# Attention of a block-sparse kernel: every unit gets its own order, and the pair items new places

## The chip, the cores and the metric

The kernel runs on one core of a Trainium2 chip. The core has TensorE (PE, with its weight loads shown apart as PEld), VectorE (DVE), ScalarE (ACT), GpSimd (POOL) and SyncE (SP, which here only issues transfers); each works through its own instructions in program order and waits for the others by semaphores. The metric is the device time of one execution in microseconds. What is compared is the median of several runs.

## The reference

The input X is 4 sequences of 2048 tokens with 256 features. It goes through an attention with 16 heads of 16 features, a layer norm, a mixture of experts and a second layer norm. Only the attention is touched:

```python
low = jnp.einsum('bnd,bmd->bnm', Qh, Kh) * SCALE          # means of blocks of 32 tokens
row_max = low.max(-1, keepdims=True)
norm = low - row_max + band * 5000.0                      # the three near blocks always
top_vals, idx = jax.lax.top_k(norm.reshape(Bm, n * n), NUM_BLOCK)   # 256 pairs a head
hi = jnp.einsum('bnqd,bnkd->bnqk', Qs, Ks) * SCALE        # chosen pairs, exactly
max_vals = full(-1e9).at[bidx, qblk].max(hi.max(-1))
attn = jnp.exp(hi - max_vals[bidx, qblk][..., None])
hi_out  = zeros.at[bidx, qblk].add(attn @ Vs)
hi_norm = zeros.at[bidx, qblk].add(attn.sum(-1))
low_attn = jnp.exp(low - row_max - 10000.0 * hi_mask) * BLK   # all other pairs, coarsely
out = (hi_out * hi_corr + low_out * low_corr) / (hi_norm * hi_corr + low_norm * low_corr + 1e-6)
```

Each head has 64 blocks of queries and of keys. The band (a block with itself and its two neighbours) holds 190 pairs, always chosen; the other 66 pairs of a head depend on the data.

## The kernel before, in words

`prepare` projects X to Q, K and V, makes the coarse scores and picks the pairs. `attend` (line 1164 on) is the attention. `experts` follows.

`attend` works on groups g = 0 to 15, each of four heads of one sequence; four groups make a batch (one sequence). A group has NU = 8 units of 256 tokens. The band is computed per unit in four steps:

- `row_max` (m, line 1294): 32 matmuls write the band's scores to `pa`, which is four PSUM banks and exists once; DVE reduces them to the maxima `m`.
- `scores` (s, line 1330), 8 units later: the scores again, turned and with the maximum subtracted by one more row of the operands, into `pa`; ACT takes the exponential into `e`. The profile calls `pa` `pm` in the first use and `ps` in the second.
- `values` (v, line 1356), one unit later: e times V into columns 0 to 255 of the bank `po`; ACT copies them to `oT`.
- `turn_values` (t, line 1378), one more unit later: two transposes of `oT` into columns 256 to 511 of `po`, and a copy from there into `ob`.

Between m and s, `lay_max` (line 1317) turns half a group's maxima (`pmt`, copied by ACT to `mt`) and SP writes them as a row into the query operand (`qt<-mt`, four transfers).

The pairs outside the band lie in OT = 9 tiles a batch, called pair tiles, k = 9 * batch + t. A pair tile passes through these items:

- `fetch` (line 1390): three gathers by POOL, of queries and keys into the one tile `gt`, of values into `gv`.
- `lay` (line 1407): SP writes each half of `gt` to DRAM (`scr`). `take` (line 1419): SP reads it back in another layout, four transfers into `qo` for part 0 and four into `kbd` for part 1. There are two sets of `qo` and `kbd`.
- `off_scores` (line 1440): two halves of 64 matmuls each into `pS`; after the second, DVE takes the maxima.
- `off_exp` (line 1464): DVE subtracts into `eo`, ACT takes the exponential in place, DVE turns the small maxima. `off_turn` (line 1478): DVE transposes `eo` to `eT`.
- `off_v` (line 1486): DVE transposes `gv` to `vt`, POOL copies it in four pieces into `vbd`.
- `off_values` (line 1496): two halves of 32 matmuls into `pO` (the same PSUM tile as `pS`), then ACT copies to `obo`, and the maxima go to a list through `pr`. `off_store` (line 1526): DVE transposes `obo` into the sums `o`.

Per group, one group later, `off_pen`, `off_scan`, `off_weights` and `off_scale` (lines 1530 to 1590) scale the pairs' sums (POOL multiplies `o`), `off_hot` (line 1591) makes the one-hot `hot` in two parts on DVE, and `off_sum` (line 1608) adds the pairs of a block by matmul (`ph`) in four parts. Two groups later `merge_exp`, `merge_weights`, `merge_band` and `merge_end` (lines 1670 to 1728) combine band, pairs and coarse part; `merge_weights` gives POOL three products over 128 x 1024, `merge_end` lets SP store the result (`att<-res`).

The order of all this is written out by hand. `plan` is a list of slots, two for each unit (TURN = 16 a group); `put` appends an item to a slot; `quiet` moves an item on past slots that hold `off_scores`. In a unit the loop at line 1833 issues m, t, the even slot (A), s, v, the odd slot (B), in this order in every unit. The items of a pair tile repeat every 7 slots with fixed distances: off_scores at 0 and 1, `take` of the tile two further on at 5 and 6, so that a tile's transfers are issued 8 slots before its off_scores. All engines receive their instructions in this one order, the transfers of SP among them.

Of the kernel before, what the change touches and what calls it, by code (L numbers as in the profile page):

```python
# [635 lines left out]
OT = (4 * NOFF + 31) // 32  # L636
# [527 lines left out]
def attend(tc, c, dram, keep, att, fills):  # L1164
# [5 lines left out]
    pe, dve, act, pool, sp = (  # L1170
        InOrder(tc, e) for e in (nc.tensor, nc.vector, nc.scalar, nc.gpsimd, nc.sync)
    )

    def matmul(*args, **kw):
        return pe.matmul(*args, start=True, stop=True, **kw)

    rows_of = [dram[n].rearrange("n (h d) q -> (n h) (d q)", d=HD) for n in ("tabq", "tabk", "tabv")]
    NU = L // 256
# [4 lines left out]
    GALL = 4 * B  # L1183
    with ExitStack() as st:
# [41 lines left out]
        NO = 2  # L1226
# [16 lines left out]
        def begin(g):  # L1243
            groups[g] = {
                "q": qts[g % NQ],
                "k": kts[g % NQ],
                "m": p3.tile([P, 2, 4, 8], F32, tag="m", name=f"m{g}"),
                "ob": p2.tile([P, 16, 4, 17], F32, tag="ob", name=f"ob{g}"),
            }
# [44 lines left out]
        def row_max(g, u):  # L1294

            s = groups[g]
            pa = ps4.tile([P, 4, 512], F32, tag="pa", name=f"pm{g}_{u}")
            for w in range(2):
                for n in range(2):
                    for j in range(4):  # L1300

                        cc = (n + j) % 2
                        t0 = 256 * u + 128 * w + 64 * cc
                        rows = slice(32 * j, 32 * j + KROWS)
                        matmul(
                            pa[64 * cc : 64 * cc + 64, j, P * w : P * w + P],
                            lhsT=s["q"][rows, t0 : t0 + 64],
                            rhs=s["k"][rows, t0 : t0 + P],
                        )
            dve.tensor_reduce(  # L1310
                s["m"][:, u // 4, :, 2 * (u % 4) : 2 * (u % 4) + 2],
                pa[:, :, 0:256].rearrange("p j (w k) -> p j w k", k=P),
                axis=AX.X,
                op=ALU.max,
            )
# [14 lines left out]
        def scores(g, u):  # L1330

            s = groups[g]
            pa = ps4.tile([P, 4, 512], F32, tag="pa", name=f"ps{g}_{u}")
            spans = [(2 * u + 1, 0, -64, 192), (2 * u + 2, 192, -64, 192)]
            n = 384
            if u == 0:
                spans.append((0, 384, 0, 128))
            elif u == NU - 1:
                spans[1], n = (2 * u + 2, 192, -64, 64), 256
            for x, o, t0, m in spans:  # L1340
                for j in range(4):
                    rows = slice(32 * j, 32 * j + KFULL)
                    matmul(
                        pa[:, j, o : o + m],
                        lhsT=s["k"][rows, P * x : P * x + P],
                        rhs=s["q"][rows, P * x + t0 : P * x + t0 + m],
                    )
            e = p3.tile([P, 4, 384], F32, tag="e", name=f"e{g}_{u}")
            act.activation(e[:, :, 0:n], pa[:, :, 0:n], AF.Exp, scale=0.25)
            s["e", u] = e  # L1350
            if u == 0:
                e0 = p1.tile([P, 4, P], F32, tag="e0", name=f"e0_{g}")
                act.activation(e0, pa[:, :, 384:512], AF.Exp, scale=0.25)
                s["e0"] = e0
# [23 lines left out]
        def turn_values(g, u):  # L1378
            s = groups[g]
            oT = s.pop(("oT", u))  # L1380
            for w in range(2):
                pe.transpose(po[:, 256 + P * w : 256 + P * w + P], oT[:, P * w : P * w + P], ident)
            dve.tensor_copy(
                s["ob"][:, 2 * u : 2 * u + 2],
                po[:, 256:512].rearrange("p (w j d) -> p w j d", w=2, j=4)[:, :, :, 0:17],
            )
# [342 lines left out]

        TURN = 2 * NU
        plan = [[] for _ in range(TURN * (GALL + 3))]

        def put(slot, f, *args):
            plan[slot].append((f, args))


        OWN = {  # L1740
            0: (0, 3, (6, 9, 10, 13)),
            1: (4, 7, (11, 14, 15, 18)),
            2: (2, 5, (9, 12, 13, 16)),
            3: (0, 3, (7, 10, 11, 14)),
        }
        for g in range(0, GALL, 4):
            z, b, i = TURN * g, g // 4, g % 4
            if g < GALL and i == 0:
                for t in range(OT):
                    k, at = b * OT + t, z + 7 * t  # L1750
                    put(at, off_scores, k, 0)
                    put(at + 2, fetch, k + NO, 0)
                    put(at + 1, off_v, k)
                    put(at + 3, fetch, k + NO, 1)
                    put(at + 1, off_scores, k, 1)
                    put(at + 2, off_exp, k)
                    put(at + 3, fetch, k + NO, 2)
                    put(at + 3, off_turn, k)
                    put(at + 4, lay, k + NO, 0)
                    put(at + 4, off_values, k, 0)  # L1760
                    put(at + 5, lay, k + NO, 1)
                    put(at + 5, off_values, k, 1)
                    put(at + 5, take, k + NO, 0)
                    put(at + 6, off_store, k)
                    put(at + 6, take, k + NO, 1)


        dense = {n for n, items in enumerate(plan) if any(f is off_scores for f, _ in items)}
# [1 line left out]
        def quiet(slot, f, *args):  # L1770
            while slot in dense:
                slot += 1
            put(slot, f, *args)
# [3 lines left out]
        for g in range(GALL + 2):  # L1777
            z, b, i = TURN * g, g // 4, g % 4
            if g < GALL:
                put(z + 11, lay_max, g, 0)  # L1780
                put(z + TURN + 2, lay_max, g, 1)

                if g + 1 < GALL:
                    for n in range(8):
                        quiet(z + n + 2, load, g + 1, n)
            if 0 < g <= GALL:
                scan, scale, at = OWN[i]
                put(z + scan, off_pen, g - 1)
                put(z + scan, off_scan, g - 1)
                put(z + scan + 1, off_weights, g - 1)  # L1790
                put(z + scale, off_scale, g - 1)
                put(z + at[0] - 2, off_hot, g - 1, 0)
                put(z + at[0] - 1, off_hot, g - 1, 1)
                for part in range(4):
                    put(z + at[part], off_sum, g - 1, part)
                if g % 2 == 1:
                    for part in range(4):
                        quiet(z + 2 + 2 * part, load_v, g - 1, 1, part)
            if g < GALL and g % 2 == 0:
                for part in range(4):  # L1800
                    quiet(z + 11 + part, load_v, g, 0, part)
            if g > 1:
                put(z + 8, merge_exp, g - 2)
                put(z + 9, merge_weights, g - 2)
                put(z + 11, merge_band, g - 2)
                quiet(z + 12, merge_end, g - 2)
            if 0 < g <= GALL:
                for cc in range(4):
                    quiet(z + 13 + cc, load_low, g - 1, cc)

        for n, f in enumerate(fills):
            quiet(TURN * 6 + n * TURN * 10 // len(fills), f, sp)

        lists = {}
        begin(0)
        patterns(0)
# [16 lines left out]
        for u in range(TURN // 2 * (GALL + 2)):  # L1833
            g = u // NU
            if u % NU == 0 and g + 1 < GALL:
                begin(g + 1)

            us, uv, ut = u - NU, u - NU - 1, u - NU - 2
            if g < GALL:
                row_max(g, u % NU)  # L1840
            if u % (4 * NU) == 0 and g < GALL:
                lists[g // 4] = p2.tile([P, OT * 32], F32, tag="r", name=f"r{g // 4}")
            if 0 <= ut < NU * GALL:
                turn_values(ut // NU, ut % NU)
            for f, args in plan[2 * u]:
                f(*args)
            if 0 <= us < NU * GALL:
                scores(us // NU, us % NU)
            if 0 <= uv < NU * GALL:
                values(uv // NU, uv % NU)  # L1850
            for f, args in plan[2 * u + 1]:
                f(*args)


NE = E - 1
# [630 lines left out]
def kernel(ctx: ExitStack, tc, x, wq, bq, wk, bk, wv, bv, *rest):  # L2486
# [24 lines left out]
    with tc.tile_pool(name="keepf", bufs=1) as kf:  # L2511
# [29 lines left out]
        with tc.If(flag == 1) as arms:  # L2541
            attend(tc, c, dram, keep, att, fills)
# [64 lines left out]
```

## Time and profile before

| what | us |
|---|---|
| runs (median; lowest, highest) | 1894.5 (1884.0, 1901.2) |
| profiled execution | 1891.8 |
| its span, first to last instruction | 1889.9 |
| busy over the span: PE, DVE, POOL, ACT | 1479.3, 1196.7, 727.0, 691.3 |
| first reduction of row maxima, last one | starts at 340.9 and 1222.2 |
| from one group's first reduction to the next, groups 1 to 14 | 51.3 to 59.2 |

A busy engine of the page is one that has an instruction in flight. In a row of groups the columns are: the engine and operation, what it writes and reads with shapes, how often, then the total busy time in us, the mean of one in ns, and the idle time just before these instructions with who ended it. A row of waits names the waiting engine and its output, whom it waited for, then us in total, how often, and the longest. Tile numbers are left out of the names, and most rows name line 654, which is the helper that keeps program order, so a group is known by its tiles.

### The profile page before, as it was taken

The numbers are of one execution on the slowest core, as the hardware profiler recorded it, in microseconds if no ns is written. First come the engines' busy times: TensorE is split into PE (matmuls) and PEld (weight loads), VectorE is DVE, ScalarE is ACT, GpSimd is POOL, SyncE is SP. The second block draws the span as 40 slices with busy tenths as digits, with TensorE's granted clock in tenths as the row PEclk, the third lists the DMA queues.
The fourth block names the chain that finished last, engine by engine and source line by source line (L and its number), as shares of the span: only waits on it lengthen the run. The fifth ranks groups of instructions, "written<-read, shape, count | busy, mean of one in ns | idle before, by whom it ended". The sixth has DMA issues, their size and how long they took to land.

```text
span 1889.9 us, 53418 instructions
## 1 busy us (share of the span) xinstructions
PE 1479.3 (78%) x21871; PEld 1064.3 (56%) x21871; DVE 1196.7 (63%) x3058; ACT 691.3 (37%) x1139; POOL 727.0 (38%) x731
## 2 busy tenths in 40 slices
PE   6787884348888778787887788863999998999980
PEld 4433442236666566566666566642557776788770
DVE  5478402537776667677776677742887558745775
ACT  3333332013333333333333333332454444544552
POOL 0100001213555535545543445333255434656355
PEclk9998997568887789898888878875999999999995
DMA  8699998668675968879788697416546565669885
GB/s 227 145 208 200 194 197 184 112 117 139 125 136 97 156 123 164 166 142 168 122 166 150 133 169 138 101 27 196 184 152 221 168 218 181 217 227 293 263 303 160
DMA packets 638763, 320.78 MB, mean 170 GB/s; under 512 B 468768, under 2 KB 601520, under 8 KB 636336
## 3 DMA queue, kind: packets, MB, share of 16 engines
q1 hardware_dynamic: 483136, 216.09, 52.0%
q0 software_dynamic: 21696, 63.50, 12.2%
q10 hardware_dynamic: 133680, 37.69, 8.6%
q8 instruction: 177, 2.90, 0.8%
q14 instruction: 74, 0.61, 0.1%
HBM read 165.33 MB, written 151.31 MB: 168 GB/s over the span
## 4 chain that ended last, share of the span: by engine, by line
PE 43%; DMA 19%; DVE 17%; issue 6%; SPq 4%; ACT 4%; POOL 3%; ACTq 3%; POOLq 0%; DVEq 0%
PE gu L654 6%; SPq L654 4%; PE po L654 4%; PE ps L654 4%; DMA tabq<-pj 3%; PE gp L654 3%; PE sy L654 3%; PE pp L654 3%; PE ph L654 3%; DVE m L654 3%; ACTq L654 3%; PE pm L654 3%; DMA vw<-v 2%; PE sT L654 2%; DMA xt<-in_L_attn_X_dram 2%
## 5 line engine op out<-in xcount | busy, mean ns | idle before, releaser
L654 ACT ACTIVATE e<-ps 128x1536 f32<-128x1536 f32 x144 | 186.2, 1304 | 299.3 <-PE ps L654 299.2
L654 POOL COPY vbd<-vt 32x512 f32<-32x512 f32 x144 | 94.2, 654 | 342.7 <-DVE vt L654 302.2
L654 DVE TENSOR_REDUCE m<-pm 128x8 f32<-128x1024 f32 x128 | 155.9, 1218 | 99.1 <-PE pm L654 98.5
L654 PE MATMUL ps<-qt,kt 26*128 26x192 f32 (+2 forms) x2176 | 151.4, 397 | 64.4 <-DVE m L654 55.5
L2250 POOL DMA_INDIRECT xs<-dx,pos x128 | 126.4, 988 | 146.5 <-issue 74.3
L654 PE MATMUL pp<-xT,wt 128*128 128x512 f32 x384 | 180.1, 617 | 3.4 <-ACT pj L654 3.4
L654 PE MATMUL gu<-guw,sxT 128*128 x736 | 176.9, 382 | 6.2 <-ACT sxT L654 4.7
L654 PE MATMUL pm<-kt,qt 25*64 25x128 f32 x4096 | 113.9, 320 | 65.9 <-ACT e L654 34.4
L654 POOL DMA_INDIRECT y<-ys,back x128 | 124.6, 974 | 105.6 <-DMA ys<-ysb 25.9
L654 PEld LDWEIGHTS ps<-qt,kt 26*128 26x128 f32 x2176 | 109.0, 220 | 94.4 <-DVE m L654 73.6
L654 PEld LDWEIGHTS gu<-guw,sxT 128*128 128x128 f32 x736 | 132.2, 191 | 25.6 <-ACT sxT L654 6.6
L654 PE MATMUL po<-e,vw 128*17 128x128 f32 (+1 forms) x4096 | 137.0, 284 | 10.4 <-issue 5.8
L654 PEld LDWEIGHTS po<-e,vw 128*17 128x17 f32 x4096 | 102.7, 111 | 51.5 <-issue 23.3
L654 PEld LDWEIGHTS pm<-kt,qt 25*64 25x64 f32 x4096 | 74.3, 152 | 95.2 <-ACT e L654 44.6
L654 PE MATMUL ph<-o,hot 128*128 128x256 f32 (+1 forms) x384 | 113.6, 431 | 16.5 <-ACT mt L654 10.5
L654 PEld LDWEIGHTS pp<-xT,wt 128*128 128x128 f32 x384 | 73.2, 200 | 84.0 <-issue 75.4
L654 ACT ACTIVATE pj<-pp,bt 128x512 f32<-128x512 f32 x96 | 65.5, 687 | 140.1 <-PE pp L654 68.4
L654 PE MATMUL pS<-kbd,qo 64*32 64x64 f32 x4608 | 71.2, 244 | 50.0 <-issue 20.0
L654 PE MATMUL sy<-dwt,shT 128*128 x368 | 97.7, 389 | 7.8 <-DVE shT L654 4.9
L654 POOL TENSOR_TENSOR o<-o,moT 128x544 f32<-128x544 f32 (+3 forms) x52 | 76.5, 1487 | 62.2 <-DMA gt<-tabq,rows 31.3
L654 ACT ACTIVATE eo<-eo 128x1024 f32<-128x1024 f32 x36 | 38.1, 1059 | 161.7 <-DVE eo L654 108.0
L654 PEld LDWEIGHTS ph<-o,hot 128*128 128x128 f32 x384 | 72.0, 203 | 38.1 <-ACT mt L654 9.2
(343 smaller groups left out, 2979.5 us busy)
## 6 DMA issues: line engine op xcount, KB each, us to landing
xr<-xs SPq DMA_DIRECT2D x92, 256.0 KB
ys<-ysb SPq DMA_DIRECT2D x92, 256.0 KB
scr<-gt SPq DMA_DIRECT2D x72, 256.0 KB
xs<-zero SPq DMA_DIRECT2D x108, 128.0 KB
qo<-scr SPq DMA_DIRECT2D x144, 64.0 KB
kbd<-scr SPq DMA_DIRECT2D x144, 64.0 KB
lt<-low SPq DMA_DIRECT2D x64, 144.0 KB
v<-vt ACTq DMA_DIRECT2D x16, 544.0 KB
```

The costliest lines, as they stand in the source:

```text
L654: return lambda *args, **kw: self.tc.keep_in_program_order(op(*args, **kw))
L2250: d = nc.gpsimd.indirect_dma_start(out=xs[i % 2], out_offset=bass.IndirectOffsetOnAxis(ap=s["pos"][:, k, t : t + 1], axis=0), in_=s["x1"][ ...
```

## The change

The instructions stay the same but for one: the copy from `po` to `ob` in `turn_values` is done by ACT in place of DVE. All else is order. Each of the 32 units of a batch has its own order of m, t, s, v, A and B (`ORDER`). The items of the nine pair tiles of a batch are put at slots listed one by one (`TILES`: off_scores twice, off_exp, off_turn, off_v, off_values twice, off_store, then three `fetch`, two `lay`, two `take` of the tile two further on). The per-group items get new slots: in `OWN`, for off_scan, off_scale, off_hot twice and off_sum four times; lay_max moves from 11 to 8 and from TURN + 2 to TURN + 1, merge_exp from 8 to 6, merge_end from 12 to 13. PSUM tiles, buffers and their numbers are unchanged.

```diff
@@ turn_values
-            dve.tensor_copy(
+            act.copy(
                 s["ob"][:, 2 * u : 2 * u + 2],
@@ attend, the plan
-        plan = [[] for _ in range(TURN * (GALL + 3))]
+        plan = [[] for _ in range(TURN * (GALL + 4))]
...
         OWN = {
-            0: (0, 3, (6, 9, 10, 13)),
-            1: (4, 7, (11, 14, 15, 18)),
-            2: (2, 5, (9, 12, 13, 16)),
-            3: (0, 3, (7, 10, 11, 14)),
+            0: (0, 3, 4, 4, 7, 10, 11, 16),
+            1: (3, 6, 7, 8, 10, 13, 16, 20),
+            2: (3, 5, 7, 8, 10, 13, 16, 19),
+            3: (1, 4, 4, 5, 9, 10, 11, 14),
         }
+        TILES = (
+            (1, 2, 2, 4, 1, 5, 6, 9, 0, 1, 3, 6, 7, 7, 8),
+            (8, 10, 10, 11, 7, 12, 13, 19, 10, 11, 11, 11, 12, 20, 21),
+            (14, 15, 16, 17, 13, 18, 19, 21, 11, 12, 20, 14, 15, 18, 19),
+            (21, 21, 24, 25, 22, 27, 27, 27, 24, 25, 32, 25, 26, 26, 27),
+            (30, 31, 32, 33, 27, 34, 34, 35, 33, 34, 34, 34, 35, 39, 40),
+            (35, 35, 37, 37, 34, 38, 39, 44, 37, 38, 37, 42, 43, 44, 45),
+            (41, 44, 44, 45, 42, 46, 47, 47, 42, 43, 50, 47, 48, 48, 49),
+            (49, 50, 51, 54, 48, 54, 55, 59, 48, 49, 50, 50, 51, 58, 59),
+            (56, 56, 57, 58, 57, 60, 61, 62, 55, 56, 68, 55, 56, 71, 72),
+        )
         for g in range(0, GALL, 4):
-                    k, at = b * OT + t, z + 7 * t
-                    put(at, off_scores, k, 0)
-                    put(at + 2, fetch, k + NO, 0)
...
-                    put(at + 6, take, k + NO, 1)
+            for t, row in enumerate(TILES):
+                k = g // 4 * OT + t
+                s0, s1, ex, tu, v, o0, o1, st_, f0, f1, f2, l0, l1, t0, t1 = (TURN * g + n for n in row)
+                put(s0, off_scores, k, 0)
+                put(s1, off_scores, k, 1)
...
-                put(z + 11, lay_max, g, 0)
-                put(z + TURN + 2, lay_max, g, 1)
+                put(z + 8, lay_max, g, 0)
+                put(z + TURN + 1, lay_max, g, 1)
...
-                put(z + at[0] - 2, off_hot, g - 1, 0)
-                put(z + at[0] - 1, off_hot, g - 1, 1)
+                put(z + hot0, off_hot, g - 1, 0)
+                put(z + hot1, off_hot, g - 1, 1)
...
-                put(z + 8, merge_exp, g - 2)
+                put(z + 6, merge_exp, g - 2)
                 put(z + 9, merge_weights, g - 2)
                 put(z + 11, merge_band, g - 2)
-                quiet(z + 12, merge_end, g - 2)
+                quiet(z + 13, merge_end, g - 2)
...
+        ORDER = (
+            "vAsBmt", "vsAtmB", "sAvtmB", "stAmvB", "mAstvB", "stAmvB", "stAmvB", "stAmvB",
+            "sAvmBt", "vmAtsB", "stAvmB", "stAmvB", "stAmvB", "stAmvB", "stAvmB", "stAmvB",
+            "sAmtvB", "stAmvB", "stAmvB", "stAmvB", "sAvtmB", "sAmtvB", "stAmvB", "stAmvB",
+            "stAmvB", "sAtmvB", "mAsvtB", "stAmvB", "mvAtsB", "stAmvB", "AsvtmB", "svmtAB",
+        )
@@ attend, the loop over units
-            if g < GALL:
-                row_max(g, u % NU)
...
-            for f, args in plan[2 * u + 1]:
-                f(*args)
+            for c_ in ORDER[u % len(ORDER)]:
+                if c_ == "m" and g < GALL:
+                    row_max(g, u % NU)
+                elif c_ == "t" and 0 <= ut < NU * GALL:
+                    turn_values(ut // NU, ut % NU)
+                elif c_ == "s" and 0 <= us < NU * GALL:
+                    scores(us // NU, us % NU)
+                elif c_ == "v" and 0 <= uv < NU * GALL:
+                    values(uv // NU, uv % NU)
+                elif c_ in "AB":
+                    for f, args in plan[2 * u + "AB".index(c_)]:
+                        f(*args)
```

## The prediction

> **What bounds the kernel now.** I read the page first, then the busy time by stretches, then the groups and waits of the steady part of the attention (460 to 1060 us), then its timeline unit by unit. The change touches only the attention, from the first `m<-pm` reduction at 341 us to about 1270 us; what lies before and behind keeps its instructions.
>
> ```profile
> span 1889.9 us, 53418 instructions
> ...
> L654 ACT ACTIVATE e<-ps 128x1536 f32<-128x1536 f32 x144 | 186.2, 1304 | 299.3 <-PE ps L654 299.2
> ```
>
> ```profile
> core 0: us, PE busy (x) PEld busy (x) DVE busy (x) ACT busy (x) POOL busy (x), PEclk, DMA share, GB/s
> 460.00:1060.00 600.00, 488.29 (x12552) 369.36 (x12548) 432.54 (x695) 207.70 (x315) 286.24 (x270) 0.86 0.78 140
> ```
>
> No engine is full: 600 us hold 87 units of 6.90 us, of which DVE works 4.97, PE 5.6, ACT 2.4. A loop through one PSUM tile is behind it. Row maxima (`pm`) and scores (`ps`) share the four banks of `pa`:
>
> ```profile
> L654 DVE TENSOR_REDUCE m<-pm 128x8 f32<-128x1024 f32 x87 | 106.0, 1219 | 60.5 <-PE pm L654 60.1
> L654 ACT COPY oT<-po 128x256 f32<-128x256 f32 x87 | 32.0, 367 | 0.6 <-PE po L654 0.5
> L654 DVE COPY ob<-po 128x136 f32<-128x136 f32 x87 | 25.0, 288 | 0.0
> L654 ACT COPY obo<-pO 128x544 f32<-128x544 f32 x25 | 15.4, 616 | 24.4 <-PE pO L654 23.6 <-PE pr L654 0.5
> ```
>
> ```profile
> PEld ps L654 <- DVE m L654: 55.7, 57, 2.5
> PE ps L654 <- DVE m L654: 42.4, 50, 2.2
> ...
> PEld pm L654 <- ACT e L654: 30.9, 34, 4.3
> ```
>
> One round is pm matmuls (0.5 us), the reduction with its hand-overs (1.55), ps matmuls (0.65), exp with hand-overs (1.9): 4.6 us; the shortest units measured are 4.5. PE's scores wait mostly for the reduction, and the reduction stands behind whatever else DVE was given. The starts of the 128 reductions show where: places 4 and 5 of each group of eight take 8.9 us on average, the other six 6.2. There merge_exp, merge_weights, the histogram work and an item of a pair tile fall together. Example, unit 36: reduction 1.22, `ob` 0.29, `vt` 1.04, pair maximum 1.20, merge_exp 2.3 (six rows), subtract and small transpose 1.42, off_sum 1.36, merge_weights 2.2 = 11.0 us, with 0.1 for each item 11.8; measured 14.6, and 12.6 as a mean over the batches.
>
> **A ledger.** For each step from one reduction to the next I add DVE's durations (plus 0.1 us an item), and the loop: pm and ps matmuls, and behind each the larger of its latency (1.55 or 1.9) and the PE work that the order puts there. The step costs the larger of the two. Units 8 to 126, before: DVE 689, loop 589, sum of the larger 739 us; measured 818. Averaged over the 32 places of a batch the ledger follows the measured times with correlation 0.82 and slope 0.76: one ledger microsecond is worth 0.76.
>
> **The change, part by part.**
>
> (a) The `ob` copy goes from DVE to ACT. DVE loses 128 x 0.288 = 36.9 us. ACT's price has no row of that shape; from `oT` (256 wide, 367 ns) and `obo` (544 wide, 616 ns) a line gives 367 - 120 x 0.865 = 263 ns, 33.7 us in all, on an engine with 4.5 of 6.9 us free. In the ledger this part alone makes 739 into 711: -28.
>
> There is a price. The Trainium skill, "PSUM — Partial Sum Buffer", section on bank collisions, says that two engines on the same bank and quadrant must be ordered even at different columns. `po` holds the values in columns 0 to 255 and the turned ones above. The trace agrees: none of 128 `ob` copies has a value matmul starting inside it, and four value blocks begin 54 ns behind the copy's end.
>
> ```profile
> who waited for it (us, times):
>   PEld ps L654: 8.8, 15
>   PEld po L654: 5.1, 4
>   PE po L654: 4.0, 2
> ```
>
> On DVE the copy stood behind the reduction; on ACT it stands behind the exp of the same unit. Where the new order puts t, then v, directly behind s (three places of 32: 4, 10, 14), the values can't run under the exp: 0.27 + 0.75 us more on the loop, 12 x 1.0 = 12 us in the ledger's sense. By the columns alone it would be 0. One of the three stands ahead of the stall in (d) and is absorbed; I take 6 (0 to 12).
>
> (b) The order within a unit. In most units s, t, A, m, v, B: t and A run under the exp, v and B under the reduction. Instructions are the same; the ledger's loop goes from 589 to 592, so by itself it is worth nothing. It also puts eo's exp behind, not ahead of, the unit's own exp in many units; that is in no sum.
>
> (c) New places for the pair items, off_hot, off_sum and merges. This spreads DVE: the excess of DVE over the loop falls from 42 to 23 us per batch of 32, old unit 36 (11.8) becomes 4.5 + 8.8 over two units. Alone, with `ob` on DVE, 739 becomes 708: -31. With (a), 675: -64, and times 0.76: **-48 us**. Ends: -33 (if DVE's total alone counts, 0.76 x 46 less the loop's 3) and -71 (the ledger's miss of 818/739 applies to both).
>
> (d) The transfers' places. Each pair tile runs gather (POOL) to `gt`, `lay` (SP) to DRAM, `take` (8 SP DMAs) into `qo` and `kbd`, then off_scores on PE. Before, take is 8 slots ahead of off_scores. Now the distances are mostly 4 to 11, but row 1 takes tile 3 at slots 20 and 21 and row 3 wants it at slot 21; row 4 to row 6 leaves one slot, row 8 to the next batch's row 1 none. Everything on PE queues behind off_scores: pm, ps, values. SP runs ahead of PE unless it waits, so each must be walked.
>
> Tile 12 (second batch; times from the start of unit 36). merge_weights leaves DVE at 5.2; POOL's three products (1.93 + 2.48 + 3.30) end at 13.0; now all of tile 12's gathers are behind them in POOL's queue, where one was ahead. Gather 1.2 + landing 4.6: 18.8. `lay` lands 4.2 later, 23.1; only then may tile 13's gather write the single `gt` (program order puts it at slot 11 too): 24.3, landed 28.9; SP has laid it at 29.7. Then SP issues 32 DMAs before tile 12 is complete: 2 vw, 3 lt, 4 qt<-mt, 8 of tile 13, 8 of tile 12, 7 loads. At 0.53 us (kbd's issue has a median of 0.486) that is 17: 46.7. The landing, by the chain in order of time:
>
> ```profile
> 643.92 6.22 DMA kbd<-scr
> ...
> 735.26 3.98 DMA qo<-scr
> ```
>
> so 51 to 53. PE arrives at 43.4 of the ledger, 48 with its usual miss: a stall of 3 to 5, and 8 to 10 if the ledger's own pace holds; I take 7. The skill's "DMA: Bandwidth & Descriptors" [...] says to issue early and wait late (rules for kernel authors)[...]. The rows of this trace have 4 to 6 with DMA at 78%, so I keep 7: three batches, **+21**. The first batch has no merges ahead: 0. Row 8's tile walks to 22 against PE's 26 behind unit 64, row 6's is early by 6: 0, no cover if SP is 4 us later than walked.
>
> (e) The head: off_scores of tile 0 now stands ahead of the first pm, which then waits for the first kbd at 347 instead of starting at 340.9; the tail's merges move by a slot. +1 (-8 to +8).
>
> Sum: -48 + 6 + 21 + 1 = -20. The profiled execution took 1891.8 us (span 1889.9 and 1.9 around it): **1871**, against a median of 1894.5 of the runs, 1.2% under it.
>
> **Rivals.**
> *No stall* (0.22): SP is early enough and banks don't show: -48 to -64 and the head's 1: 1829 to 1845. For it: in the steady part PE never waited for kbd. Against: distances were 8 slots.
> *Only the copy pays* (0.22): DVE's order is not the limit; the queues wait for each other. (a) gives 0.76 x 28 = -21, costs 6 + 21 + 1: 1899. For it: `issue` gaps on PE up to 4.9 us and a ledger short by 79 us.
> *Slower, by the transfer wait* (0.25): at slot 21 of each batch PE stops for longer, since SP falls behind (its waits for gathers and mt were up to 9.2 us in the steady part), and rows 6 and 8 join. The gain of 42 is gone at 10.5 us a batch; with 7 + 7 + 4 = 18 it is +30 and the head's 1: 1923.
> *Likeliest* (0.31): 1871, own range 1855 to 1885.
>
> **Numbers.** About 1% is what a measurement of this kernel can tell from no change, so faster means under 1875.5. The likeliest case gives 0.24 faster, 0.07 same; no stall 0.22 faster; only the copy 0.02 faster, 0.15 same, 0.05 slower; the wait 0.03 same and 0.22 slower. Sum: 0.48, 0.25, 0.27. Range 1832 (no stall, the upper end of (c) in part) to 1920 (the slower rival's middle).
>
> **What would show it.** The `ob` row on ACT near 0.26 us. Reductions' mean distance near 6.7 us (6.87 before), places 4 and 5 near 7.9 in place of 8.9: (c). PE's wait for kbd or qo near 21 us in three places, unit 10 of a batch: (d). `po` waiting for ACT `ob`: (a). Wrong if the distances don't even out, if pS waits for DMAs over 40 us, or if ACT's queue becomes what pm waits for (over twice its 31 us).

## The result, and the profile after

| | median us (lowest to highest, runs) |
|---|---|
| before | 1895.9 (1884.0 to 1901.2, 4) |
| after | 1964.7 (1962.2 to 1970.6, 4) |
| after / before | 1.0377, 95% interval 1.0321 to 1.0432 |

The change costs 69 us by the medians, 3.8% by the ratio. The ratios in this document and their intervals are worked out from the single runs of a kernel, without the slow ones, and so can differ by some tenths of a per cent from what two medians give. The prediction was 1871, with a range up to 1920: wrong in sign, and the time lies outside its range.

The profiled execution of the changed kernel took 1967.0 us, 75.2 more than the one of before. Its page, in the same order as before (columns: busy us and mean ns, then the idle time ahead):

```profile
span 1965.3 us, 53254 instructions
...
L654 ACT ACTIVATE e<-ps 128x1536 f32<-128x1536 f32 x144 | 186.7, 1308 | 294.6 <-PE ps L654 294.6
...
L654 PE MATMUL pS<-kbd,qo 64*32 64x64 f32 x4608 | 77.5, 253 | 149.4 <-DMA kbd<-scr 115.8
```

The exp row is what it was. The last row is the new one: PE stood 115.8 us ahead of off_scores, waiting for `kbd`. Not all of that is new: 35.3 of it is the start of the attention, where PE waited for other loads before, and 18.6 is one wait at unit 7, where PE before waited 11.6 for `low`. In the units from the ninth reduction on it is 60.1, and 0 before. The steady stretch (460 to 1060 us):

```profile
core 0: us, PE busy (x) PEld busy (x) DVE busy (x) ACT busy (x) POOL busy (x), PEclk, DMA share, GB/s
460.00:1060.00 600.00, 460.29 (x11473) 346.92 (x11456) 388.84 (x555) 212.97 (x365) 260.56 (x249) 0.82 0.76 131
```

```profile
L654 DVE TENSOR_REDUCE m<-pm 128x8 f32<-128x1024 f32 x79 | 96.3, 1219 | 52.4 <-PE pm L654 51.8
L654 ACT COPY oT<-po 128x256 f32<-128x256 f32 x80 | 29.6, 370 | 92.7 <-PE po L654 91.1 <-PE pm L654 1.5
L654 ACT COPY ob<-po 128x136 f32<-128x136 f32 x78 | 21.0, 269 | 20.1 <-PE po L654 19.9
```

```profile
PE pS L654 <- DMA kbd<-scr: 37.5, 7, 15.2
PEld ps L654 <- DVE m L654: 28.3, 30, 2.5
PE ps L654 <- DVE m L654: 22.0, 20, 2.3
PEld pm L654 <- ACT e L654: 15.6, 26, 1.4
PE po L654 <- ACT ob L654: 15.1, 17, 1.7
```

In 600 us 79 reductions start, where there were 87. The two waits that the change was forecast to shorten did shorten: PE's for the reduction from 42.4 to 22.0, its weight loads' for the exp from 30.9 to 15.6. The copy, now on ACT, has its own waiters over the whole attention:

```profile
who waited for it (us, times):
  PEld po L654: 34.3, 28
  PE po L654: 31.9, 32
```

**Where 75 us went.** I add PE's busy time (matmul or weight load) and its gaps over 0.1 us between the ninth and the last reduction, by who ended the gap. `issue` marks a gap for which the profile names nobody. The last two columns are profiles of two experiments below, taken on one chip.

| us | before | after | before again | takes early, again |
|---|---|---|---|---|
| execution | 1891.8 | 1967.0 | 1886.6 | 1909.0 |
| first reduction at | 340.9 | 345.1 | 340.5 | 348.2 |
| ninth to last reduction | 817.9 | 891.5 | 814.3 | 831.9 |
| PE busy | 665.8 | 686.1 | 659.7 | 680.6 |
| PE idle | 152.1 | 205.4 | 154.3 | 151.4 |
| of it pS for `kbd` | 0 | 60.1 | 0 | 0 |
| ps for the reduction | 55.5 | 32.1 | 62.9 | 27.1 |
| pm for the exp | 34.8 | 14.4 | 36.0 | 13.7 |
| po for `ob` | 0 | 24.3 | 0 | 25.0 |
| po for `oT` | 0 | 12.3 | 0 | 12.9 |
| pS and ps, `issue` | 23.5 | 33.7 | 18.6 | 44.8 |

Of the 73.6 us more in this stretch 53.3 are idle time and 20.3 are PE's own longer duration for the same matmuls.

**The stall, tile 12.** Timeline of the changed kernel, first the steps issued by SP, then PE, DVE and ACT around the stop (start, duration, engine, instruction, and in brackets the idle time ahead):

```profile
641.21 3.31 SPq L654 DMA_DIRECT2D scr<-gt  x2
...
650.07 2.70 SPq L654 DMA_DIRECT2D qt<-mt  x4
653.19 1.95 SPq L654 DMA_DIRECT2D qo<-scr  x4
...
661.07 2.01 SPq L654 DMA_DIRECT2D qo<-scr  x4
...
665.91 3.46 SPq L654 DMA_DIRECT2D kbd<-scr  x4
```

```profile
673.72 0.39 PE L654 MATMUL pS<-kbd,qo 64*32 64x64 f32 x2 [12.75 <-DMA kbd<-scr]
675.32 2.02 PE L654 MATMUL pS<-kbd,qo 64*32 64x64 f32 x126 [1.22 <-DMA kbd<-scr]
...
679.01 1.45 ACT L654 ACTIVATE e<-ps 128x1536 f32<-128x1536 f32 x1 [18.64 <-PE ps L654]
```

The order of events is the one walked. PE is free at 660.97, the last `kbd` transfer is issued by 669.4 and the data come at 675.3. ACT's exp then starts 18.6 us after its last work: all of the unit queues behind off_scores.

What made SP late shows in its waits between 644 and 670 us, and in the chain of work that ends at PE's restart (start, duration):

```profile
SPq L654 <- ACT ob L654: 2.6, 1, 2.6
SPq L654 <- DMA qo<-scr: 2.3, 4, 0.8
SPq L654 <- PE po L654: 1.7, 2, 1.3
```

```profile
662.07 6.99 DMA qo<-scr
669.08 6.11 DMA kbd<-scr
675.19 0.14 issue
675.32 2.07 PE pS L654 x116
```

The first wait stands ahead of `qt<-mt`. In the second SP waits for the landing of its own earlier transfers: the last three issues of `kbd` each start 0.01 to 0.02 us after the landing of the transfer that was issued eight earlier. So two landings, 7.0 and 6.1 us, stand one behind the other ahead of PE. The 3.46 of the row `kbd<-scr x4` above is 1.3 of issuing and 2.2 of this wait (the fourth of these waits comes after it).

### The profile page after: what moved, and what is told of

Read it like the earlier page. It is cut to its first block, busy times and chain, and to the rows that moved or that the text cites. A ratio compares the mean times of both kernels' runs of the same rounds, so it can differ in the third digit from the quotient of the medians.

```text
span 1965.3 us, 53254 instructions
## 1 busy us (share of the span) xinstructions
PE 1501.4 (76%) x21871; PEld 1078.1 (55%) x21871; DVE 1176.2 (60%) x2930; ACT 727.0 (37%) x1267; POOL 724.1 (37%) x731
## 4 chain that ended last, share of the span: by engine, by line
PE 46%; DVE 17%; DMA 17%; ACT 6%; issue 5%; SPq 4%; ACTq 3%; POOL 1%; another core or an unknown queue 0%; POOLq 0%; DVEq 0%
PE gu L654 6%; PE ps L654 6%; PE po L654 5%; PE ph L654 4%; SPq L654 4%; PE gp L654 3%; PE pm L654 3%; PE sy L654 3%; PE pS L654 3%; ACTq L654 3%; DVE m L654 3%; DMA kbd<-scr 3%; ACT e L654 3%; PE pp L654 2%; DMA tabq<-pj 2%
## 5 line engine op out<-in xcount | busy, mean ns | idle before, releaser
L654 PE MATMUL pS<-kbd,qo 64*32 64x64 f32 x4608 | 77.5, 253 | 149.4 <-DMA kbd<-scr 115.8
L654 PE MATMUL ps<-qt,kt 26*128 26x192 f32 (+2 forms) x2176 | 158.6, 410 | 41.2 <-DVE m L654 31.9
L654 PEld LDWEIGHTS pS<-kbd,qo 64*32 64x32 f32 x4608 | 60.3, 119 | 167.1 <-issue 132.8
L654 PEld LDWEIGHTS ps<-qt,kt 26*128 26x128 f32 x2176 | 114.1, 229 | 65.3 <-DVE m L654 42.0
L654 PEld LDWEIGHTS po<-e,vw 128*17 128x17 f32 x4096 | 101.7, 110 | 73.1 <-ACT ob L654 33.7
L654 PE MATMUL ph<-o,hot 128*128 128x256 f32 (+1 forms) x384 | 123.4, 466 | 0.5 <-DVE oo L654 0.4
L654 DVE TENSOR_REDUCE r<-pS 128x32 f32<-128x1024 f32 x36 | 43.9, 1219 | 129.1 <-PE pS L654 129.1
L654 PEld LDWEIGHTS pp<-xT,wt 128*128 128x128 f32 x384 | 73.6, 201 | 83.2 <-issue 77.2
L654 ACT COPY oT<-po 128x256 f32<-128x256 f32 x128 | 47.3, 370 | 144.3 <-PE po L654 142.6
```

Of the source, the lines that this page charges most:

```text
L654: return lambda *args, **kw: self.tc.keep_in_program_order(op(*args, **kw))
```

## The experiments

All times are medians, with the ratio to the kernel before on the same chip. Order only, places only, places and copy and the first no bank wait came from a chip on which the kernel before took 2020.3; there only the ratios say something.

### The transfers: taken away, and put in alone

**Takes early**: the changed kernel, with the takes of rows 1, 4 and 8 back at 4 to 12 slots ahead of their use.

```diff
-            (8, ..., 12, 20, 21),
+            (8, ..., 12, 13, 14),
...
-            (30, ..., 35, 39, 40),
+            (30, ..., 35, 36, 37),
...
-            (56, ..., 56, 71, 72),
+            (56, ..., 56, 60, 61),
```

> The changed kernel, with the takes of three pair tiles moved back to just behind their lays (row 1 from slots 20, 21 to 13, 14; row 4 from 39, 40 to 36, 37; row 8 from 71, 72 to 60, 61); nothing else. Transfer theory (PE stands at off_scores because its takes are issued too late): the 49 us at unit 10 of the four batches and the 10 us at unit 4 go, the time is 1965 - 59 = about 1905 and PE's wait for kbd in the steady part is under 5 us. Rival, order theory (the loss is in the new order and places themselves, the wait only shows where they queue): the wait turns up behind another releaser and the time stays above 1945.

Measured 1907.8, ratio 1.0073 (1.0041 to 1.0105). PE's wait for `kbd` in the units is gone. So the late takes cost 57 of the 69 us, as the transfer theory had it.

**One take late**: the kernel before, with only the takes of one tile per batch moved to the place that row 1 has.

```diff
-                    put(at + 5, take, k + NO, 0)
+                    put(at + 13 if t == 1 else at + 5, take, k + NO, 0)
-                    put(at + 6, take, k + NO, 1)
+                    put(at + 14 if t == 1 else at + 6, take, k + NO, 1)
```

> The kernel before with only one take a batch issued late: the tile of row 3 gets its take at slots 20 and 21, its off_scores is at 21 and 22 as before. Transfer theory: PE waits for kbd or qo at unit 10 of each batch, some 8 to 14 us each, +30 to +55, 1925 to 1950. Rival (SP runs ahead, the slot of a take does not matter by itself): within 10 us of 1895.

Measured 1962.8, ratio 1.0388 (1.0313 to 1.0462): +73 us by the ratio, more than was expected of it. Its waits of PE, 460 to 1060 us:

```profile
PE ps L654 <- DVE m L654: 40.8, 48, 2.4
PE pS L654 <- DMA kbd<-scr: 37.4, 4, 18.0
```

Two of the four stops fall in this stretch, up to 18 us each. The wait for the reduction stays as it was: a stall adds to the other waits, it doesn't absorb them. One tile of nine, two lines, costs as much as the whole change.

### The copy alone, in both orders

**Copy on ACT**: the kernel before, only the engine of the copy changed. **Copy on DVE**: the changed kernel with the copy put back.

```diff
-            dve.tensor_copy(
+            act.copy(
```

> The kernel before with only the ob copy moved from DVE to ACT. My ledger: 28 us of it times 0.76, -21, so about 1875; the old order has scores, values and turns in places where the copy stands ahead of the next exp, so few bank waits. Rival (the copy on ACT is what costs, by the bank po and by ACT's queue): slower than before, +10 to +30.

> The changed kernel with the ob copy back on DVE. Transfer theory: the stalls at unit 10 stay; the 33 us of PE waits for the copy go, but DVE gets 37 us back, so between 1945 and 1975. Rival (the copy on ACT is the main cost): 1965 - 33 = 1932 or less.

Copy on ACT: 1889.2, ratio 0.9978 (0.9950 to 1.0007): no gain that can be told from none, where the ledger had 21 us, and no loss as the rival had it. Copy on DVE: 1986.4, ratio 1.0538 (1.0448 to 1.0628); its median is 21.6 us above the change's. Neither theory had that number. In its waits of PE the wait for the copy has grown past that for the reduction:

```profile
PE po L654 <- DVE ob L654: 24.5, 21, 2.8
PE ps L654 <- DVE m L654: 20.1, 20, 3.6
```

So of these two orders the copy's engine matters in the new one, where v can stand close behind t. The wait for `ob` comes with that order, and there ACT is the better engine; it isn't a price of ACT, as step (a) had it.

### Order and places, each without the other

**Order only**: the kernel before with the loop over `ORDER`. **Places only**: takes early, with the old order and the copy on DVE. **Places and copy**: takes early, with the old order.

```diff
# order only, on the kernel before
-            if g < GALL:
-                row_max(g, u % NU)
...
+            for c_ in ORDER[u % len(ORDER)]:
# places only, on takes early
-            act.copy(
+            dve.tensor_copy(
...
+        ORDER = ("mtAsvB",)
# places and copy, on takes early
+        ORDER = ("mtAsvB",)
```

> The kernel before with the new order within the units alone (old places of all items, copy of ob on DVE). With late takes undone the changed kernel still was 14 us slower than before, where the ledger gave it 48 less. Theory A (the order costs: values wait for the ob copy in the bank po, turns for oT): slower than before by 20 to 40, with PE waits for ob and oT of 35 or more. Theory B (the order helps as meant, the places cost): faster than before by 5 to 20. The ledger gives 0.

> New places of all items with the three takes early, old order m t A s v B in every unit, ob on DVE. Theory A (the places help, the order costs): faster than before by 10 to 24 (the ledger's 31 times 0.76). Theory B (the places cost): slower by 10 to 40. The waits of the scores for the reduction should be below the 55 us of before in both.

> New places with the three takes early and ob on ACT, old order m t A s v B: the changed kernel less its order and its late takes. Theory A (the order costs): 1870 to 1880, 30 us under the 1908 of the kernel with the new order. Theory B (order and places belong together, the places were made for this order): 1908 or more.

Ratios: order only 1.0474 (1.0400 to 1.0548), places only 1.0443 (1.0356 to 1.0530), places and copy 1.0406 (1.0340 to 1.0471). The ledger gave 0, -31 and -64. The theories that order or places cost had the direction, with 10 to 40 us, less than half of what came. Places only, which should have relieved the wait for the reduction, has a large one (waits of PE, 460 to 1060 us; the kernel before, on another chip, had 42.4):

```profile
PE ps L654 <- DVE m L654: 56.9, 43, 5.1
PE pm L654 <- ACT e L654: 36.1, 26, 4.2
```

Together, with the takes early, the same parts stand at 1.007 to 1.011 on other chips, and at 1.0175 on this one (no bank wait, below). Order and places are fitted to each other: either alone is 4% to 5% slower. Their effects don't add, and the ledger, which adds them, has the wrong sign for two of them. How much of this is the wait and how much the clock is not separated: the mean granted clock of the runs is 0.821 to 0.823 in these three, 0.832 in no bank wait and 0.846 in the kernel before.

### What is left of the forecast gain

**Before again** and **takes early, again**: two kernels from above, unchanged, on one chip, for a pair of profiles.

> The kernel before, unchanged, run as one of the set so that its trace comes from the same chip as the others: ratio 1.00 within 1%.

> The changed kernel with the three takes early once more, for a trace beside that of the kernel before on one chip. Clock theory of what is left: PE waits as long as before (150 us, units 8 to 126), but 20 to 30 us more of the stretch are PE's own work at the half clock; 0.7% to 1.5% over before. Rival (waits): PE's idle time is the larger by 15 or more, its busy time equal.

Measured 1888.7, ratio 0.9989 (0.9963 to 1.0014), and 1913.4, ratio 1.0108 (1.0078 to 1.0139): what the clock theory expected. The table above has their columns; here the windows (columns as above) and the waits of PE, first of before again, then of takes early:

```profile
460.00:1060.00 600.00, 484.64 (x12641) 367.71 (x12640) 442.05 (x699) 206.86 (x313) 286.09 (x273) 0.86 0.80 141
```

```profile
PE ps L654 <- DVE m L654: 46.6, 56, 2.4
PE pm L654 <- ACT e L654: 25.4, 18, 5.4
PE pS L654 <- issue: 17.2, 13, 4.2
```

```profile
460.00:1060.00 600.00, 491.27 (x12353) 371.45 (x12353) 410.69 (x598) 230.69 (x396) 276.85 (x266) 0.84 0.78 141
```

```profile
PE pS L654 <- issue: 24.6, 15, 4.0
PE ps L654 <- DVE m L654: 20.7, 21, 2.2
PE po L654 <- ACT ob L654: 17.9, 19, 1.8
PE ps L654 <- issue: 10.5, 5, 3.1
PE po L654 <- ACT oT L654: 9.8, 12, 1.1
PE pm L654 <- ACT e L654: 9.8, 17, 1.1
```

The gain is there: over the units 58 us less wait for the reduction and the exp (62.9 + 36.0 against 27.1 + 13.7), ten more than the forecast 48 (against the first profile of before it is 50). Nearly all of it is given back by waits that stood below these: `issue` ahead of pS and ps, `ob`, `oT`. Idle time is 154.3 and 151.4. On top PE takes longer for its instructions: 484.64 us over 12641 is 38.3 ns, 491.27 over 12353 is 39.8, with the granted clock at 0.84 in place of 0.86. That is 21 us over the units. The rest is the start, 7.7 us later at the first reduction.

The packets of the trace tell more of the `issue` gaps. Between the ninth and the last reduction queue 8, of the kind "instruction", moved these (transfers, MB, share of the DMA engines), in before again and in values twice on before (below):

```profile
q8 instruction: 134, 2.20, 1.4%
```

```profile
q8 instruction: 163, 2.67, 1.6%
```

That is one transfer of 16 KB for about 257 instructions of PE in both, so the queue loads PE's instructions. In takes early 22 of the 27 `issue` gaps over 1 us end 0.9 to 2.1 us after such a load has come in; by chance 5 would, and of the 34 gaps as long whose releaser is named 4 do. The 22 make 45 us; in before again it is 12 of 15 gaps and 18 us. So PE likely waits for its own instructions there, and this is about half of the some 55 us given back. No run varied the loading alone.

**No bank wait**: takes early, where v no longer follows t ahead of m in places 10 and 14 (slot A stands between them) or stands directly behind t in place 4; places 16 and 21 still have v directly behind t. Run once beside order only and once more.

```diff
-            "vAsBmt", "vsAtmB", "sAvtmB", "stAmvB", "mAstvB", ...
-            "sAvmBt", "vmAtsB", "stAvmB", "stAmvB", "stAmvB", "stAmvB", "stAvmB", ...
+            "vAsBmt", "vsAtmB", "sAvtmB", "stAmvB", "mAsvtB", ...
+            "sAvmBt", "vmAtsB", "stAmvB", "stAmvB", "stAmvB", "stAmvB", "stAmvB", ...
```

> The changed kernel with takes early, and at the three places where t, then v, stand directly behind s (4, 10, 14) the values moved ahead of the turn or behind m. Bank theory: PE's waits for the ob copy fall from 22 to 33 us to about half, the time from 1908 to 1890 to 1898. Rival (the wait for the copy is only where PE waits for ACT's exp anyway): within 5 us of 1908.

> Takes early and no value block behind such a copy, once more on this chip, to stand beside the other two: bank theory 1.000, rival (waits only move from the copy to the exp) 1.007 to 1.011 as with the takes alone.

Ratios 1.0175 (1.0099 to 1.0250) and 1.0094 (1.0063 to 1.0126). The first lies above both of its theories, the second fits the rival. The second profile has 8.9 us of waits for `ob` in the steady stretch in place of 17.9, and 14.7 for the exp in place of 9.8, 12.9 for `oT` in place of 9.8. The wait moved; the time stayed within the noise (1.0094 against 1.0108).

**Halves apart**: takes early, with the two halves of off_scores that shared a slot in rows 3, 5 and 8 put into neighbouring ones (off_exp of row 8 one slot on). **All mended**: no bank wait and halves apart together, and the old order in the first eight units.

```diff
# rows 3, 5, 8 of halves apart; all mended has them too
-            (21, 21, 24, ...), (35, 35, 37, ...), (56, 56, 57, ...)
+            (21, 22, 24, ...), (35, 36, 37, ...), (56, 57, 58, ...)
# all mended
-            for c_ in ORDER[u % len(ORDER)]:
+            for c_ in ORDER[u % len(ORDER)] if u >= NU else "mtAsvB":
```

> The changed kernel with takes early, and the two halves of off_scores of rows 3, 5 and 8 in neighbouring slots instead of one (off_exp of row 8 one slot on). Supply theory (128 small matmuls in a row run PE out of instructions; that is the issue gap ahead of pS, 34 us against 17 before): these gaps fall to about 20, the time by 10 to 17 us, to a ratio near 1.002. Rival (the gaps come from elsewhere): they stay at 30 or more and the ratio stays at 1.007 to 1.011.

> All mends together: takes early, no value block behind a copy that stands behind an exp, halves apart, and the old order in the first eight units (where only row maxima and pair tiles run; the first row maxima came 7 us later in the new order). If what was given back was given back by these four, the waits for the reduction stay low and the time is 20 to 40 us under the kernel before. Rival (a wait taken from one place turns up at the next): within 10 us of before.

Measured 1913.6, ratio 1.0134 (1.0073 to 1.0196), and 1914.9, ratio 1.0149 (1.0093 to 1.0205). Halves apart has 24.5 us of `issue` gaps ahead of pS where takes early had 33.9, and 8 us of a wait (ph for DVE's `oo`) where takes early had 0.9: the supply theory had the gaps nearly right, and the time not. All mended has its first reduction at 341.8, one us behind the kernel before, has 9.2 us of waits for `ob` over the units in place of 25.0, and is no faster; with +24 us it also lies above what its rival allowed. Each of three mends shortened its wait, and none brought the time down.

### Is PE's own work on the path?

**Values twice**: the matmuls of `values` are issued a second time, with the same result, in the kernel before and in takes early.

```diff
-            for r, (x, mine, next_) in enumerate(parts):
+            for r, (x, mine, next_) in 2 * list(enumerate(parts)):
```

> The kernel before with every block of value matmuls issued twice (the second writes the same results), which fills PE's waits with work and adds 128 x 0.75 = 96 us of it at full clock. Clock theory (the half clock is granted for gaps in PE's work, and costs more than they do): time at half clock falls by 80 us or more and the time rises by less than 15 us or falls. Rival (the clock is a by-product): +17 us by the ledger to +96 us if all of it lies on the path, the share of half clock as before.

> The same doubling of the value matmuls in the changed kernel with takes early, where they lie under the reduction. Clock theory: half clock falls by 80 us or more, the time by 0 to 25 us. Rival: +27 us by the ledger to +96 us.

On before: 1969.9, ratio 1.0432 (1.0367 to 1.0496), +82 us. On takes early: 1973.0, ratio 1.0425 (1.0357 to 1.0494), +60 over takes early on the same chip. In before PE is busy 82.5 us more between the ninth and the last reduction (742.2 against 659.7) and idle for 151.9 against 154.3: all that was added to PE came out as time. In takes early PE is busy 50 us more (730.7) and idle 15 more (166.7), and the stretch is 66 longer. The ledger, in which DVE and the loop hide such work, had 17 and 27. That PE's clock would rise with the fuller queue and pay for it is out too: PE was at half clock for 229 us against 235 in before, and in takes early for 192 against 282, and that kernel still became slower.

## Why the prediction was wrong

**(d), the transfers: the right mechanism, the wrong size.** +21 was forecast, 57 measured by taking it away. Of tile 12's walk, counted from the start of unit 36 (615.2), PE's arrival was 45.8 for a forecast 48, the landing 5.9 us behind the last issue as taken, and `lay` of tile 13 ended at 29.3 for 29.7. The term that failed is the 17 us for 32 DMAs at 0.53 us, with no wait of SP in it: from 644.5 to 669.4 SP needed 24.9 for exactly these 32. Without its waits an issue took some 0.57, near the 0.53; 6.5 us SP waited, 2.6 ahead of `qt<-mt`, 1.7 for PE, and 2.2 for its own earlier `qo` transfers to land. The stall was 14 and not 7. So one stop costs twice as much, and it was counted three times. The first batch was priced at 0, since no merges are ahead, and has 10.2; the four stops at place 10 make about 50 us. Row 8's tile, priced at 0 with a cover of 4 us, was late at place 4 in three batches, another 10. The prediction's own sign, wrong if pS waits for DMAs over 40 us, came true with 60.1. The rule of the Trainium skill that was weighed there ("DMA: Bandwidth & Descriptors", rules for kernel authors), to issue early and wait late, agrees with one take late, +73 us for 8 slots; how early is enough depends here on SP's waits.

**(a) to (c), the ledger: the forecast of the waits held, the conversion into time failed.** Without (d) the sum was -41 (-48, 6 for the bank, 1 for the head); with the transfers mended the measurement says +14 to +20. The failing term is the slope, "one ledger microsecond is worth 0.76". It was fitted over the 32 places of one kernel, so it tells which units are long, not what happens when one is made shorter. As a price it failed every test: the copy -21 forecast and -4 measured, with an interval that holds 0 (copy on ACT); the places -31 in the ledger and +4.4% measured; the order 0 and +4.7%; PE's added work 17 and 82. The prediction's own sign for (c) failed as well. The mean of places 4 and 5 went from 8.7 us to 8.2 between the paired profiles, and the other six rose from 6.2 to 6.6; over the 32 places the spread of the distances grew from 1.6 to 2.8, a part of which is only that m moves within the unit.

What the runs show in its place is PE's queue. Its idle time in the stretch stayed between 150 and 156 us in before, in takes early and in each of its mends, whichever wait was shortened. It has many causes, and our reading is that each releaser found late is followed by the next one, little later. Values twice and one take late show the same from the other side: whatever is put into PE's queue, work or stall, comes out nearly whole at the end.

**(a), the bank.** The size of the copy was right (269 ns for 263). Its price was forecast at 0 to 12, 6 taken; 24 us of waits appear in that row. No bank wait shows that it is no cost of that size: halved, it returns at the exp and `oT`.

**(b) and (e).** Order by itself was "worth nothing": it is worth +4.7% in the old places. The head: +4.2 for +1, within its bounds.

**The rivals.** The slower one named the mechanism and the places that decided, at 18 us a batch where PE's waits at places 10 and 4 are about 15, but set the ledger's gain of 42 against it. Without that gain its numbers give 1964 (1891.8 + 4 x 18); that this is close to the measurement is two misses that cancel, the waits smaller and the rest of the change at +14 to +20 instead of 0. "Only the copy pays" was right that queues waiting for each other make the ledger void, and wrong that the copy pays.

**Open.** The 21 us that PE needs more for the same matmuls go with the half clock, 282 us of it against 235. In the second profile of no bank wait the half clock lasted 228 us, PE was busy for 662.3 and idle for 155.5, and the stretch took 818.7: near before again (659.7, 154.3, 814.3). The single runs say the same: the mean granted clock is 0.854 in takes early, again and 0.864 in the runs of before beside it, and within each of the two a run with 0.01 more clock is 14 and 11 us faster. By these slopes, an estimate, 11 to 14 of the 19 us between them belong to the clock. Why the new order gets less of it is open; no kernel here varied the clock alone. What in takes early could be changed so that PE's instructions come in time is open too. No version tried beats the kernel before; copy on ACT is level with it.

## What to carry to other kernels

When a transfer is given a new slot, count what the issuing queue has to work off ahead of it, with its waits, those for its own earlier transfers among them, and compare that with the arrival of the in-order engine that stops for it; one tile out of nine, 8 slots too late, cost 3.9%. A sum of durations per step that follows one kernel's timeline doesn't price a change to it: test the price first by adding a known amount of work to the engine that the sum calls hidden. Gaps ahead of long runs of small matmuls can be the loading of instructions: look at the instruction queue's packets. Where order and places were fitted to each other, judge them together, and when a wait is shortened, look for the one that stands right behind it.

## What was not expected of the hardware

The granted clock in the records is full or half, in steps of some 3.4 us. In before 37 of 38 returns to full clock had at most 0.3 us of PE idle time in the 3.4 us ahead; ahead of the drops it was 1.7 us on average, from 0.6 to 3.2, so gaps that fill a part of such a step were enough to lose the clock. The Trainium skill, "TensorE: Matmul & The Clock Gate", gives gaps above some 3.4 us as the plain rule (section on oscillation in real kernels); what it says of small idles between groups (second failure mode) is nearer to this trace. An issue on SP has a median of 0.49 us for `kbd`; in the stretch ahead of the stall 32 issues took 0.78 each with SP's waits, and some 0.57 without.
